# Two transfers per expert chunk move to GpSimd's queue, and three results of the RWKV projections are read one to three turns later

## The chip, the cores and the metric

The kernel runs as one program on one core of one Trainium2 chip. The metric is device time in microseconds of one execution, smaller being better; several executions are timed and their median is given. The engines are named as in the profile: PE (matmul), PEld (its weight loads), DVE, ACT, POOL (GpSimd) and SP; "PEq", "SPq" and so on are their instruction queues.

## The reference

Two transformer-like layers over x of shape (8, 512, 256), float32: eight sequences of 512 tokens with 256 channels. Only the first layer is touched by the change. Cut to what matters:

```python
x = L0_attn_x
xn = _layernorm(x)
x = x + rwkv(xn) + moe(xn)          # layer 0
xn = _layernorm(x)
x = x + attn(xn) + ffn(xn)          # layer 1

def rwkv(x):                        # B=8, T=512, D=256, 16 heads of 16
    dx = conv3(x) - x
    t5 = tanh((x + dx * maa_x) @ maa_w1).reshape(B, T, 5, 32)
    m = einsum('btfc,fcd->fbtd', t5, maa_w2)
    xw, xk, xv, xr, xg = [x + dx * (maa_i + m[i]) for i in range(5)]
    r, k, v, g = xr @ Wr, xk @ Wk, xv @ Wv, silu(xg @ Wg)
    w_log = -exp(time_decay + tanh(xw @ decay_w1) @ decay_w2)
    # S = exp(w)*S + k v^T forward in time, the mirrored recurrence backward
    y = forward_scan(r, k, v, w_log) + backward_scan(r, k, v, w_log)
    y = y * sigmoid(dx @ gate_w + gate_b)
    return group_norm(y) * g @ Wo

def moe(x):                         # 8 experts, 2 per token, hidden 704
    scores = x @ Wg.T
    top, idx = top_k(scores, 2)
    y_e = (silu(x @ W1[e].T) * (x @ W2[e].T)) @ W3[e].T
    return sum of y_e over the token's two experts, times its score
```

## The kernel before, in words

Layer 0 and layer 1 run one after the other; each has its own on-chip pools. In both, the order of the work on PE, DVE, ACT and SP is written out by hand: pieces of work are Python generators, and `Turns.turn()` steps every running generator once, up to its next `yield`. What a generator emits in one turn is put behind what the others emitted in the same turn, and each engine carries its instructions out in that order. A bare `yield` therefore emits nothing and puts all that follows in this generator one turn later, relative to the other generators. POOL alone is not pinned: a scheduler orders its instructions.

Layer 0 begins with `norm_and_route(b)` for the eight sequences (layer norm, router scores, top two), beside `projections(0)`. `place()` then computes for each token its two rows in a table `slots` in DRAM, grouped by expert and cut into 39 chunks of 256 rows, and `scatter()` writes the normalised tokens there with 64 indirect transfers from POOL.

After that three kinds of generators run side by side.

- `scans(turns)` sets the number of turns. It goes over the eight sequences `b`, two channel halves `c` and eight value groups `vg`: 128 steps of four turns each, 512 turns. A step works on a tile `kv` of 128 partitions by 2 by 512: multiply by k (L688), for each of the two values one forward scan (L699) and one backward scan (L703) along time, multiply by r (L708), all on DVE, and, for two steps together, a matmul on PE that sums over the key rows into `ys` (L714). The `kv` tile is loaded by `spread` (L665): eight transfers on SP's queue that read value rows from the DRAM tile `vd` and repeat each on 16 partitions. `kv` has four buffers, and the transfers for step n+1 are written into the program at the start of step n.
- `projections(b + 1)` is added when sequence b begins its scans, and must have filled `made[b + 1]` when they end. It loads the normalised, transposed tokens `xnT` (L485, SP), waits three turns, forms `dx` on DVE (L514 to L516), then projects on PE. `v` goes to DRAM (`vd`, L591, ACT's queue). For the decays, ACT computes `d = exp(-exp(w))` (L620, L621). DVE forms `q = d*d - 1` from it (L626, L627), ACT a first value `near` of 1/q by Ln and Exp (L634, L636), and DVE one Newton step, `dq` (L640, L641), which is scaled (L645, L646). For b of 2 and more, the addition of x in `mixed` (L572) is done on POOL.
- `then(scatter(), experts())`: 32 turns of scatter, then 39 chunks of twelve turns. A chunk gathers expert weights with two indirect transfers from POOL: `wgu` (two buffers) and `wdn` (one buffer). Its tokens `xs` come from `slots` (L396, `load_slots`), are transposed on PE (`turned`, L405) and copied by ACT (`xsT`, L418). PE makes the gate and up products `g` and `u` (L426), ACT applies Silu (L452), DVE multiplies (L435), and PE makes `y` (L465). ACT copies `y` to `ys` (L472), and L473 writes it to the DRAM table `outs`.

`ending(b, c)` normalises and gates the `ys` of a half sequence and, for the second half, multiplies by Wo, adds x and stores it.

Before the change the loads of `xs` are on SP's queue and the stores of `ys` on ACT's queue. In the compiled program the transfers of SP and ACT together take eight completion semaphores in rotation, and those of POOL eight others; a transfer that takes a semaphore first waits until the transfer that had it before has landed. Layer 1, which begins when layer 0's last store has landed, gathers the rows of `outs` per token.

Of the kernel before, what the change touches and what calls it, by code (L numbers as in the profile page):

```python
# [165 lines left out]
def two_layers(ctx: ExitStack, tc: tile.TileContext, a: dict, out: bass.AP):  # L166
    nc = tc.nc
    vec_e, act_e, pool_e, pe = nc.vector, nc.scalar, nc.gpsimd, nc.tensor
# [70 lines left out]
    with ExitStack() as l0:  # L239
# [146 lines left out]
        def weights(i, name, of, n, bufs):  # L386
            w = ew.tile([P, n], F32, tag=name, name=f"{name}_{i}", bufs=bufs)
            pool_e.indirect_dma_start(
                out=w, out_offset=None, in_=of,
                in_offset=bass.IndirectOffsetOnAxis(ap=wrow[:, i : i + 1], axis=0),  # L390
            )
            return w

        def load_slots(i):
            xs = ex.tile([P, NS, D], F32, tag="xs", name=f"xs_{i}", bufs=2)
            nc.sync.dma_start(  # L396
                xs, slots[i * CH : (i + 1) * CH].rearrange("(n p) d -> p n d", p=P)
            )
            return xs

        def turned(i, xs):
            ps = ps_gu.tile([P, NC, CH], F32, tag="gu", name=f"xsT_{i}")
            for c in range(NC):
                for n in range(NS):
                    pe.transpose(  # L405
                        ps[:, c, n * P : (n + 1) * P], xs[:, n, c * P : (c + 1) * P], ident
                    )
            return ps

        def experts():  # L410
            nxt = weights(0, "wgu", a["w0_gu"], GU0, 2)
            ps = turned(0, load_slots(0))
            yield
            for i in range(NCH):
                w, xps = nxt, ps
                wd = weights(i, "wdn", a["w0_dn"], DN0, 1)
                xT = ex.tile([P, NC, CH], F32, tag="xT", name=f"xsT_{i}", bufs=1)
                act_e.copy(xT, xps)  # L418
                if i + 1 < NCH:
                    nxt = weights(i + 1, "wgu", a["w0_gu"], GU0, 2)  # L420
                    xs = load_slots(i + 1)
                yield

                def hidden(o, at):
                    for c in range(NC):
                        pe.matmul(  # L426
                            o, w[:, at + c * P : at + (c + 1) * P], xT[:, c, :],
                            start=c == 0, stop=c == NC - 1,
                        )

                hs = [hpool.tile([P, 2, CH], F32, tag="h", name=f"h_{i}_{j}") for j in range(3)]

                def product(j, g, u):
                    n = 2 - j // 2
                    vec_e.tensor_tensor(hs[j][:, :n, :], hs[j][:, :n, :], u[:, :n, :], ALU.mult)  # L435
                    if n == 1:
                        o = hs[j][64:, 1, :]
                        vec_e.tensor_tensor(o, o, g[64:, 1, :], ALU.mult)

                last = None  # L440
                for j in range(3):
                    g = ps_gu.tile([P, 2, CH], F32, tag="gu", name=f"g_{i}_{j}")
                    hidden(g[:, 0, :], 4 * j * D)
                    hidden(g[:, 1, :], (4 * j + 2) * D)
                    yield
                    if last:
                        product(j - 1, *last)
                    u = ps_gu.tile([P, 2, CH], F32, tag="gu", name=f"u_{i}_{j}")
                    n = 2 - j // 2
                    for k in range(n):  # L450
                        hidden(u[:, k, :], (4 * j + 2 * k + 1) * D)
                    act_e.activation(hs[j][:, :n, :], g[:, :n, :], AF.Silu)  # L452
                    if n == 1:
                        act_e.activation(hs[j][64:, 1, :], g[:64, 1, :], AF.Silu)
                    last = g, u
                    yield
                if i + 1 < NCH:
                    ps = turned(i + 1, xs)
                product(2, *last)
                yield  # L460
                y = ps_gu.tile([P, NS, D], F32, tag="gu", name=f"y_{i}")
                for n in range(NS):
                    for j in range(NJ0 + 1):
                        lo = 64 * (j == NJ0)
                        pe.matmul(  # L465
                            y[:, n, :], hs[j // 2][lo:, j % 2, n * P : (n + 1) * P],
                            wd[lo:, j * D : (j + 1) * D], start=j == 0, stop=j == NJ0,
                        )
                        if j % 3 == 2:
                            yield  # L470
                ys = ex.tile([P, NS, D], F32, tag="ys", name=f"ys_{i}", bufs=1)
                act_e.copy(ys, y)  # L472
                act_e.dma_start(  # L473
                    outs[i * CH : (i + 1) * CH].rearrange("(n p) d -> p n d", p=P), ys
                )

# [3 lines left out]
        def projections(b):  # L480
# [5 lines left out]
                xnT[:, :, PAD : PAD + T], lines[b].rearrange("(c p) t -> p c t", p=P)  # L486
            )
            xT = [xnT[:, c, PAD : PAD + T] for c in range(NC)]
            for _ in range(3):
                yield  # L490

            def shifted(c, s):
# [2 lines left out]
            def big(tag, bufs=2):  # L495
                return rw.tile([P, NC, T], F32, tag=tag, name=f"{tag}_{b}", bufs=bufs)
# [123 lines left out]
                act_e.activation(dT[:, co, :], pss[co], AF.Exp, bias=V("time_decay", co))  # L620
            act_e.activation(dT, dT, AF.Exp, scale=-1.0)  # L621
            yield


            q = rw.tile([P, NC, T + 1], F32, tag="v", name=f"q_{b}", bufs=2)
# [8 lines left out]
                act_e.activation(near[c], q[:, c, :T], AF.Ln, scale=-1.0)  # L634
            for c in range(NC):
                act_e.activation(near[c], near[c], AF.Exp, scale=-1.0)  # L636
            yield
            dq = big("dq")
            for c in range(NC):
# [34 lines left out]
        def scans(turns):  # L674
# [4 lines left out]
            for n, (b, c, vg) in enumerate(todo):  # L679
                if c == vg == 0:  # L680
                    x = rw.tile([P, NT, D], F32, tag="x", name=f"x_{b}")
                    z = rw.tile([P, NC, T], F32, tag="z", name=f"z_{b}")
                    if b + 1 < B:
                        turns.add(projections(b + 1))
# [102 lines left out]
        for b in range(B):  # L787
            nc.sync.dma_start(xns[b], tokens(a["x"][b]))
        turns = Turns()
        first = projections(0)  # L790
        for b in range(B):
            turns.add(norm_and_route(b))
# [10 lines left out]
        place()  # L803
        turns.finish()
        turns.add(then(scatter(), experts()))
        for _ in scans(turns):
            turns.turn()
# [616 lines left out]
```

## Time and profile before

| | us |
|---|---|
| median of 3 runs | 2783.87 |
| lowest and highest | 2782.39, 2789.58 |
| the profiled execution, its time | 2787.46 |
| its span, first to last instruction | 2785.7 |
| PE, PEld, DVE busy | 2359.8, 1402.9, 2137.6 |
| ACT, POOL busy | 870.1, 407.2 |
| mean granted PE clock | 0.919 of full |

The profiled execution's own time is 1.8 us over its span and 3.6 us over the median. The scans and experts of layer 0 fill about 150 to 1480 us of the span, layer 1 the rest from about 1500 us. A busy share is an average over these stages; what a wait in one of them is worth is read from that stage alone.

### The profile page before, as it was taken

The page shows a single profiled execution, that of the slowest core. Times are in us where ns is not written, and L with a number is a line of the kernel's source. Part 1 is how long each engine was busy: PE and PEld are TensorE (multiplying, and loading weights), DVE is VectorE, ACT ScalarE, POOL GpSimd, SP SyncE. Part 2 cuts the span into 40 slices and gives each one's busy share as a digit, 9 for nine tenths or more (in the row PEclk, how much of TensorE's full clock was granted, in tenths as well). Part 3 has the DMA queues.
Part 4 walks back from the last instruction along what each step waited for, and adds up shares of the span by engine and source line. Part 5 has one row for each costly group of instructions (what it writes and reads, how often), then busy time and mean ns, then how long its engine had stood idle before and what let it go on. Part 6 is the DMA issues. An engine that isn't in the chain of part 4 may idle for free.

```text
span 2785.7 us, 32431 instructions
## 1 busy us (share of the span) xinstructions
PE 2359.8 (85%) x11772; PEld 1402.9 (50%) x11772; DVE 2137.6 (77%) x3042; ACT 870.1 (31%) x1649; POOL 407.2 (15%) x368
## 2 busy tenths in 40 slices
PE   4756888988989889898873899999999989998996
PEld 3313555545555555555651445655555545555554
DVE  4698989899999899889894866667576676667656
ACT  1203231232312323122110234444333434343344
POOL 0074121221212112121102110001010100001000
PEclk8768998999999999999895899999998999999998
DMA  8245454445454444544543100010010100000000
GB/s 281 76 147 168 136 169 130 149 131 168 147 164 136 147 149 145 170 118 149 165 128 140 54 28 24 9 35 28 20 31 31 31 28 27 28 20 28 20 9 16
DMA packets 123886, 263.22 MB, mean 94 GB/s; under 512 B 25264, under 2 KB 76368, under 8 KB 118608
## 3 DMA queue, kind: packets, MB, share of 16 engines
q1 hardware_dynamic: 86912, 129.58, 16.4%
q0 software_dynamic: 17376, 103.69, 11.2%
q10 hardware_dynamic: 19440, 27.87, 2.7%
q8 instruction: 95, 1.56, 0.2%
q14 instruction: 63, 0.52, 0.1%
HBM read 215.17 MB, written 45.88 MB: 94 GB/s over the span
## 4 chain that ended last, share of the span: by engine, by line
PE 49%; DVE 26%; DMA 6%; ACT 4%; issue 3%; SPq 2%; POOL 1%; DVEq 0%; ACTq 0%; POOLq 0%
PE y L1307 6%; PE g L1261 5%; PE u L1261 5%; PE y L465 4%; DVE kv L699 4%; PE g L426 3%; DVE kv L703 3%; DMA kv<-vd 3%; PE sc_g L1159 2%; PE u L426 2%; PE o_g L1187 2%; PE ys L714 2%; SPq L665 2%; DVE kv L688 2%; PE qkv_l L1051 1%
## 5 line engine op out<-in xcount | busy, mean ns | idle before, releaser
L703 DVE TENSOR_TENSOR_SCAN kv<-d,kv 128x512 f32<-128x512 f32 x256 | 336.9, 1316 | 8.8
L699 DVE TENSOR_TENSOR_SCAN kv<-dq,kv 128x512 f32<-128x512 f32 x256 | 320.4, 1252 | 2.5
L426 PE MATMUL g<-xsT,wgu 128*128 128x256 f32 x936 | 249.3, 413 | 32.0 <-ACT xsT L418 31.9
L465 PE MATMUL y<-wdn,h 128*128 128x256 f32 x936 | 259.3, 416 | 11.9 <-DVE h L435 11.9
L1167 ACT ACTIVATE pt_g<-sc_g 128x512 f32<-128x512 f32 (+1 forms) x384 | 171.0, 531 | 237.4 <-PE sc_g L1159 202.8
L426 PEld LDWEIGHTS g<-xsT,wgu 128*128 128x128 f32 x936 | 188.3, 207 | 112.1 <-ACT xsT L418 51.4
L465 PEld LDWEIGHTS y<-wdn,h 128*128 128x128 f32 x936 | 173.8, 200 | 111.1 <-issue 76.7
L1261 PE MATMUL g<-xT,w 128*128 128x512 f32 x384 | 199.6, 645 | 24.4 <-DVE h L1296 9.4
L1261 PE MATMUL u<-xT,w 128*128 128x512 f32 x384 | 190.1, 618 | 18.7 <-DVE h L1296 7.6
L426 PE MATMUL u<-xsT,wgu 128*128 128x256 f32 x780 | 192.8, 387 | 0.0
L714 PE MATMUL ys<-kv,cst 128*32 128x512 f32 x512 | 122.1, 638 | 78.3 <-DVE kv L708 78.1
L688 DVE TENSOR_TENSOR kv<-kv,k 128x1024 f32<-128x1024 f32 x128 | 158.1, 1236 | 37.8 <-DMA kv<-vd 22.0
L1307 PE MATMUL y<-w,h 128*128 128x256 f32 x768 | 179.3, 385 | 0.0
L426 PEld LDWEIGHTS u<-xsT,wgu 128*128 128x128 f32 x780 | 151.6, 196 | 37.9 <-issue 14.8
L708 DVE TENSOR_TENSOR kv<-kv,r 128x1024 f32<-128x1024 f32 x128 | 160.8, 1257 | 3.7
L1279 DVE TENSOR_TENSOR h<-h,u 128x512 f32<-128x512 f32 x96 | 66.0, 688 | 120.5 <-PE u L1261 115.9
L1307 PEld LDWEIGHTS y<-w,h 128*128 128x128 f32 x768 | 141.7, 190 | 32.2 <-issue 9.5
L452 ACT ACTIVATE h<-g 128x512 f32<-128x512 f32 (+1 forms) x117 | 61.6, 526 | 287.8 <-PE g L426 280.2
L1173 DVE TENSOR_TENSOR pt_g<-pt_g,cst 128x512 f32<-128x512 f32 x128 | 85.2, 686 | 69.6 <-ACT pt_g L1167 69.5
L1261 PEld LDWEIGHTS g<-xT,w 128*128 128x128 f32 x384 | 72.5, 202 | 108.3 <-issue 83.9
L1167 ACT ACTIVATE pt_l<-sc_l 128x384 f32<-128x384 f32 (+1 forms) x256 | 98.0, 469 | 90.0 <-PE sc_l L1159 71.9
L1173 DVE TENSOR_TENSOR pt_l<-pt_l,cst 128x768 f32<-128x768 f32 (+1 forms) x128 | 107.9, 885 | 14.8 <-ACT pt_l L1167 14.8
(296 smaller groups left out, 3763.4 us busy)
## 6 DMA issues: line engine op xcount, KB each, us to landing
kv<-vd SPq DMA_DIRECT2D x1024, 64.0 KB, 2.7
cb<-cd SPq DMA_DIRECT2D x128, 128.0 KB, 2.9
slots<-zero SPq DMA_DIRECT2D x1, 9984.0 KB, 35.4
xs<-slots SPq DMA_DIRECT2D x39, 256.0 KB, 4.8
outs<-ys ACTq DMA_DIRECT2D x39, 256.0 KB, 2.1
w<-in_w ACTq DMA_DIRECT2D x12, 384.0 KB, 9.5
xn<-in_x SPq DMA_DIRECT2D x8, 512.0 KB, 8.7
xnT<-xT ACTq DMA_DIRECT2D x16, 256.0 KB, 2.1
```

What stands on the lines that cost most here:

```text
L426: pe.matmul(o, w[:, at + c * P : at + (c + 1) * P], xT[:, c, :], start=c == 0, stop=c == NC - 1,)
L465: pe.matmul(y[:, n, :], hs[j // 2][lo:, j % 2, n * P : (n + 1) * P], wd[lo:, j * D : (j + 1) * D], start=j == 0, stop=j == NJ0,)
L688: vec_e.tensor_tensor(kv, kv, bc(kc, 1, NV), ALU.mult)
L699: vec_e.tensor_tensor_scan(out=kv[:, i, :], data0=qc, data1=kv[:, i, :], initial=0.0, op0=ALU.mult, op1=ALU.add,)
L703: vec_e.tensor_tensor_scan(out=kv[:, i, ::-1], data0=dc[:, ::-1], data1=kv[:, i, ::-1], initial=0.0, op0=ALU.mult, op1=ALU.add,)
L708: vec_e.tensor_tensor(kv, kv, bc(rc, 1, NV), ALU.mult)
L714: pe.matmul(y[r0 : r0 + 32, :], C["take"][:, 24 - 8 * at : 56 - 8 * at], kv[:, i, :], start=at == 0, stop=at == 3, skip_group_check=True,)
L1167: act_e.activation(pt[:, i, :end], scs[i][:, :end], AF.Exp, scale=0.25)
L1173: vec_e.tensor_tensor(pt[:, :, a0 : a0 + m], pt[:, :, a0 : a0 + m], bc(mask[:, :m], 1, 4), ALU.mult,)
L1261: pe.matmul(ps, w[:, k, c * P : (c + 1) * P], xT[:, c, :], start=c == 0, stop=c == NC - 1,)
L1279: vec_e.tensor_tensor(hs[-1], hs[-1], u, ALU.mult)
L1307: pe.matmul(y[:, i, :], hs[k][:, (t + i) * P : (t + i + 1) * P], w1[j - 5 + k][:, 2, :], start=k == 0, stop=k == 5,)
```

## The change

Three things are edited, all in layer 0.

1. `load_slots` and the store of `ys` to `outs` are issued by POOL in place of SP and ACT: 39 transfers each.
2. `projections` waits six turns, not three, after it asks for `xnT`, for every sequence but the first.
3. One more `yield` stands between the computation of `d` on ACT and `q` on DVE, and one more between `near` on ACT and the Newton step on DVE.

All arithmetic is the same. `projections(b)` has 41 yields before and 46 after (43 for the first sequence).

```diff
@@ load_slots
             xs = ex.tile([P, NS, D], F32, tag="xs", name=f"xs_{i}", bufs=2)
-            nc.sync.dma_start(
+            pool_e.dma_start(
                 xs, slots[i * CH : (i + 1) * CH].rearrange("(n p) d -> p n d", p=P)
             )
@@ experts
                 act_e.copy(ys, y)
-                act_e.dma_start(
+                pool_e.dma_start(
                     outs[i * CH : (i + 1) * CH].rearrange("(n p) d -> p n d", p=P), ys
                 )
@@ projections
             xT = [xnT[:, c, PAD : PAD + T] for c in range(NC)]
-            for _ in range(3):
+            for _ in range(6 if b else 3):
                 yield
...
             act_e.activation(dT, dT, AF.Exp, scale=-1.0)
             yield
+            yield
...
             q = rw.tile([P, NC, T + 1], F32, tag="v", name=f"q_{b}", bufs=2)
...
             for c in range(NC):
                 act_e.activation(near[c], near[c], AF.Exp, scale=-1.0)
+            yield
             yield
             dq = big("dq")
```

In the instruction lists of the changed program SP has 39 transfers fewer and ACT 39 fewer, and ACT has four fewer loads of a function table (75 for 79). POOL's scheduler puts the new transfers into its queue in a fixed pattern per chunk: the `wdn` of chunk i, the store of chunk i-1, the `wgu` of chunk i+2, the `xs` of chunk i+3. Layer 1's instructions on ACT and DVE are in the same order as before.

## Prediction

> **What bounds the kernel now.** I read the stages first: busy time of each engine in four windows.
>
> ```profile
> core 0: us, PE busy (x) PEld busy (x) DVE busy (x) ACT busy (x) POOL busy (x), PEclk, DMA share, GB/s
> 0.00:240.00 240.00, 134.65 (x368) 63.77 (x368) 175.07 (x322) 45.83 (x64) 86.66 (x84) 0.74 0.47 162
> 240.00:1480.00 1240.00, 1067.33 (x4078) 666.48 (x4078) 1125.34 (x1114) 312.07 (x483) 219.27 (x163) 0.93 0.49 147
> ```
>
> All edits act in the second window, 1240 us long. DVE is the fullest engine there (91%), PE second (86%); POOL and ACT are mostly idle. DVE's idle time, 1240 - 1125 = 115 us, is what can be won while DVE leads. The waits of DVE in that window name 94 us of it:
>
> ```profile
> DVE kv L688 <- DMA kv<-vd: 22.0, 13, 5.0
> DVE kv L688 <- DMA xs<-slots: 15.7, 5, 5.1
> DVE q L626 <- ACT d L621: 11.1, 5, 3.8
> DVE dx L514 <- DMA xnT<-xnT: 10.9, 2, 6.4
> DVE dq L640 <- ACT near L636: 10.7, 6, 2.2
> DVE x L782 <- PE o L777: 8.8, 8, 2.4
> DVE xf L568 <- PE m L563: 8.3, 1, 8.3
> ```
>
> The numbers are total us, times, longest. L688 does not read xs: where it is said to wait for xs, that transfer sat ahead of the kv transfers on SP, so both kv rows are one wait, 37.7 us. Why is kv late? The waits of SP's queue say:
>
> ```profile
> SPq L665 <- DMA outs<-ys: 389.2, 32, 26.0
> SPq L665 <- PE ys L714: 119.0, 26, 16.2
> SPq L396 <- DMA outs<-ys: 70.6, 7, 14.9
> ```
>
> A kv load has nothing to do with the expert output; it waits for it because both rotate through the same eight semaphores. The chain of waits, in order of time, shows one whole case:
>
> ```profile
> 806.04 1.70 PE y L465 x6
> ...
> 807.77 0.59 ACT ys L472
> ...
> 808.38 2.08 DMA outs<-ys
> ...
> 810.48 0.30 SPq L665
> ...
> 810.82 4.18 DMA kv<-vd
> ...
> 815.13 1.24 DVE kv L688
> ```
>
> So once per chunk the scans on DVE hang on the end of PE's expert product, and PE in turn waits for the scans (PE ys L714 on DVE kv L708: 70 us, 36 times). The two fullest engines are tied in a ring.
>
> **What the Trainium skill says.** "DMA: Bandwidth & Descriptors", section "Issuing engines are not separate DMA queues": transfers from SP, ACT and GpSimd run on the same 16 DMA engines, so moving one saves issue time, not bandwidth. The trace fits: DMA share is 0.49, no limit. "SBUF — State Buffer", section "SBUF: two separate sides": a transfer issued by GpSimd has its descriptors written by GpSimd, through a port pair that it shares with DVE, and a holder keeps the pair for a whole instruction. The trace agrees for POOL's arithmetic: beside the POOL addition at 596.45 a scan took 1.93 us, not the median 1.22. It shows nothing of it for POOL's indirect transfers: beside the wgu issue at 615.36 (1.64 us long) DVE's operations keep 1.22 and 0.42. A plain POOL transfer of 256 rows is not in this trace.
>
> **The change part by part.**
>
> *xs and outs leave SP's and ACT's rotation.* SP loses both rows of waits on outs, and 39 issues of 0.42 us. Left in SP's rotation beside kv are vd, xnT, x and after, four transfers per sequence. SP may then run as far ahead as free kv buffers allow: the spread for step n+1 reuses the buffer of step n-3, whose sums were emitted at step n-1 or n-2, and eight issues plus landing take 8 x 0.42 + 2.7 = 6.1 us of a 10.4 us step (512 turns over 147 to 1480 us are 2.6 us each). The waits on vd (48.6 us) and on x (45.0 us, before the store of after) remain on SP with kv queued behind them; each is at most 12 us, about one step, against a lead of one to two steps. Of the 37.7 us I leave 4: 34 won.
>
> *ACT* drops 39 issues of 0.366 us between the copies ys and xsT. PE waits for xsT 24 times, 31.9 us; at some 0.4 us each that falls by 10. It is on the path only where PE leads: credited to PE's slack below, not to the sum.
>
> *POOL* gets 78 issues. The nearest rows, indirect transfers of 128 rows, take 0.94 to 1.94 us each; for 256 rows I bound by 0.94 and twice 1.94, and take the 1.3 of wgu and wdn: 78 x 1.3 = 101 us (73 to 303), inside POOL's 1240 - 219 = 1021 idle us. The store waits for ACT's ys copy; queued behind it are wgu of chunk i+2, xs of chunk i+3, and sometimes an addition xf, a z product or the xnT pads. In front of it stands wdn, which already waits for the same y on PE (377.8 us, 37 times), so the added wait is the copy, 0.6 us, and the issue. wgu is needed 17 turns (44 us) later and lands in 7.8; xs is asked a chunk earlier than before. Only xf can be felt: PE waits for it 5.6 us now, and two turns of cover lie between; an added 3 us fits into 5. What the issues take from DVE is bounded by 0 (an issue that doesn't touch DVE; nothing here could make DVE faster) and 0.7 each, the stretch beside an addition: 0 to 55 us. I take 0, by the wgu issue above.
>
> *First chunk.* xs of chunk 0 now stands behind wdn on POOL. Both lie on the chain at 237 us (scatter, xs, first transposes), where PE stood 14.5 us for it: one issue ahead and its own 1.3 cost +2.5.
>
> *Three extra turns before dx* (10.9 us won of 10.9, the waits being 6.4 and 4.5 against 7.8 of cover). The xnT transfer itself is also freed from the outs waits.
>
> *One turn between d and q, one between near and dq.* Longest waits 3.8 and 2.2, cover 2.6: of 21.8 us I leave 3, so 19 won. Nothing is added to any engine. PE and ACT get the final segments of projections(b) later, turn 46 of 64; the next sequence's first kv is emitted at turn 60, so nobody waits. In the first sequence the two yields fit into the existing turns but for the Silu, which falls behind place(): nothing.
>
> *Sum of DVE waits removed*: 34 + 11 + 19 = 64. Then what is late next: PE. Its own needs in the window are 1067 busy plus its waits that are not on DVE, 31.9 - 10 + 14.5 + 9.5 + 5.6 + 1 = 53: 1120. DVE's are 1240 - 64 = 1176. PE's slack against DVE falls from 120 to 56, about half. DVE's present waits on PE, without the single 8.3 at the first chunk, are 15.7; I take them as doubling with the halved slack: -16. Net 64 - 16 - 2.5 = 45.5. The profiled execution is 2785.7 + 1.8 = 2787.5, so 2742 for a like one; against the median, 2783.9 - 45.5 = **2738**. Layer 1 is emitted as before: 0.
>
> **The rivals.**
>
> *PE takes over.* The clock column is 0.88 to 0.97 in parts of the window, so PE's 1067 is partly slow clock; if in-order PE gives back 40 of 64, the gain is 22: 2762. Against: where PE is densest (510 to 670) the clock is 0.97, as in layer 1, so denser is not slower.
>
> *The kv waits have another origin* (PE ys, 119 us, or vd): then only the turns win, 30 less 8 less 2.5: about 20, 2764. Against: the chain above, and the same steps at 363, 595, 626, 1161 and 1382 us.
>
> *POOL's issues stretch DVE* (slower). 78 plain transfers at 0.7 us of locked-out DVE, as with POOL's additions, are 55 us on the leading engine: 45.5 - 55 = 9 lost, 2793. It decides from 45.5 / 78 = 0.58 us per issue. For: the skill's shared pair, 256 rows where I have only seen 128. Against: the undisturbed operations at 615.
>
> *The whole 64 is kept*, PE's clock rising with its density: 2722.
>
> **How the numbers follow.** 2738 has 0.52, the fully kept gain 0.12, PE 0.15, another origin 0.08, POOL's stretch 0.13. A measurement of this kernel can tell about 0.3%, 8 us. Of the 0.23 for the two small gains 0.02 falls within 8 us, of the 0.13 for the stretch 0.03: faster 0.85, same 0.05, slower 0.10. The range goes from 2706 (every named DVE wait gone, 94, less the 16 given back: 78 won) to 2779 (the small gains at their worst); the stretch is left outside with a little at the lower end.
>
> **What would show it.** Right: no wait of SP on outs; SP's longest rows are PE ys, DVE x and vd; L688's waits under 8 us in all; L626, L640 and L514 near zero; DVE's share in the window up from 91 to about 94%; DVE's waits on PE some 15 us longer. POOL's issues 1 to 2 us. Wrong: scans (L699, L703) with means above 1.32 and 1.25 us; kv waits left; PE waits on POOL xf well over 5.6; or wgu or wdn awaited by PE at all.

## The result and the profile after

The changed kernel takes **2761.84 us** (median of 6 runs, 2756.70 to 2770.33) against 2785.2 us before (6 runs): ratio **0.9919, 95% interval 0.9898 to 0.9939**. It was measured a second time beside the experiments, with 0.9884 (0.9867 to 0.9901), 2759.8 against 2792.1 us. So it is 23 to 32 us faster, where 45.5 were forecast. The direction was right; the gain was half of the forecast by the first measurement and 0.7 of it by the second. As the experiments show, the sum holds two errors that partly cancel: one of its steps, the three turns before `dx`, does not win 10.9 us but costs some 30, and the others win more than forecast.

The window 240 to 1480 us of the changed kernel, columns as in the same view of before:

```profile
240.00:1480.00 1240.00, 1067.90 (x4106) 670.79 (x4104) 1141.72 (x1125) 311.71 (x490) 279.54 (x239) 0.93 0.48 145
```

DVE went from 1125 to 1142 us of 1240, that is 92% and not 94%. POOL has 60 us more. Of the tiles named below, `h` is the experts' product of gate and up, `xf` a mixed input of the projections, `yg` the gated sums of a half sequence, `sd` and `z` belong to its normalisation, and `x` is the sum that `ending` stores. What DVE waits for in this window (total us, times, longest), first rows:

```profile
DVE x L784 <- PE o L779: 24.3, 10, 4.4
DVE h L435 <- PE u L426: 22.3, 5, 14.4
DVE yg L736 <- PE ys L716: 14.6, 9, 2.0
DVE kv L690 <- DMA kv<-vd: 13.9, 4, 5.6
DVE sd L757 <- ACT sd L755: 5.0, 1, 5.0
DVE dq L642 <- ACT near L637: 2.5, 1, 2.5
```

The rows for q and dx are gone, dq is down to one wait. But kv still waits 13.9 us, in four places, and two rows stand high that were next to nothing before: h (2.5 before) and yg (0.5 before). (Of x and sd, some 13 us lie after the last scan, which now comes earlier and so pulls the tail into this window.) What SP's queue waits for:

```profile
SPq L667 <- PE ys L716: 403.7, 59, 27.9
SPq L787 <- DVE x L784: 151.5, 8, 46.0
SPq L667 <- DMA kv<-vd: 89.5, 91, 3.8
SPq L667 <- DMA vd<-v: 76.7, 6, 17.4
```

Both rows on outs (389 and 71 us) have vanished, as said. The last row, six waits on the store of vd, the longest 17.4 us, comes up again below.

In the following, "the scans" are the stretch from the first kv product (L688) to the last (L708): 1330.6 us before, 1313.3 in the changed kernel. The rest after it (1302 to 1312 us in all kernels) is left alone by every edit.

### The profile page after: what moved, and what is told of

It is laid out like the page before. It is cut to its first block, busy times and chain, and to the rows that moved or that the text cites. A ratio compares the mean times of both kernels' runs of the same rounds, so it can differ in the third digit from the quotient of the medians.

```text
span 2768.6 us, 32498 instructions
## 1 busy us (share of the span) xinstructions
PE 2354.6 (85%) x11772; PEld 1404.0 (51%) x11772; DVE 2146.9 (78%) x3042; ACT 861.1 (31%) x1645; POOL 466.3 (17%) x446
## 3 DMA queue, kind: packets, MB, share of 16 engines
q0 software_dynamic: 23616, 124.14, 13.9%
## 5 line engine op out<-in xcount | busy, mean ns | idle before, releaser
L705 DVE TENSOR_TENSOR_SCAN kv<-d,kv 128x512 f32<-128x512 f32 x256 | 335.9, 1312 | 8.8
L701 DVE TENSOR_TENSOR_SCAN kv<-dq,kv 128x512 f32<-128x512 f32 x256 | 328.1, 1282 | 2.7
L690 DVE TENSOR_TENSOR kv<-kv,k 128x1024 f32<-128x1024 f32 x128 | 166.1, 1298 | 13.9 <-DMA kv<-vd 13.9
L1169 ACT ACTIVATE pt_l<-sc_l 128x384 f32<-128x384 f32 (+1 forms) x256 | 98.0, 470 | 90.1 <-PE sc_l L1161 71.9
```

The lines of the kernel that those rows point to most:

```text
L690: vec_e.tensor_tensor(kv, kv, bc(kc, 1, NV), ALU.mult)
L701: vec_e.tensor_tensor_scan(out=kv[:, i, :], data0=qc, data1=kv[:, i, :], initial=0.0, op0=ALU.mult, op1=ALU.add,)
L705: vec_e.tensor_tensor_scan(out=kv[:, i, ::-1], data0=dc[:, ::-1], data1=kv[:, i, ::-1], initial=0.0, op0=ALU.mult, op1=ALU.add,)
L1169: act_e.activation(pt[:, i, :end], scs[i][:, :end], AF.Exp, scale=0.25)
```

## The experiments

Each was timed in five rounds; those run together share the runs of the kernel before (medians of 2784.8 to 2792.1 us). The table is what the text below refers to. "DVE free" is the scans' length less DVE's busy time in it; "kv" and "yg" are DVE's waits there. yg counts the waits for PE's sums and includes one of 2.0 us in the tail after the last scan, except for before and e2; one more wait of yg per trace, for which the trace names no cause, is not in it: 9.6 us in e8, 4.3 in e6, 2.5 in e7. The 26.4 of e5 hold one wait of 10.5 at the first chunk.

| kernel | ratio to before (95%) | scans, us | DVE free | kv | yg |
|---|---|---|---|---|---|
| before | 1 | 1330.6 | 116.6 | 37.7 | 0.5 |
| changed | 0.9919 (0.9898-0.9939) | 1313.3 | 90.1 | 13.9 | 14.6 |
| e8 changed again | 0.9884 (0.9867-0.9901) | 1308.7 | 86.2 | 14.2 | 14.6 |
| e1 transfers alone | 0.9866 (0.9845-0.9888) | 1303.2 | 83.1 | 0 | 2.8 |
| e2 turns alone | 1.0010 (0.9992-1.0028) | 1341.5 | 124.3 | 54.4 | 11.2 |
| e11 outs alone | 0.9875 (0.9851-0.9900) | 1298.9 | 79.1 | 0 | 3.2 |
| e5 transfers + three turns | 0.9926 (0.9908-0.9944) | 1312.8 | 92.8 | 14.6 | 26.4 |
| e12 transfers + one turn before dx | 0.9861 (0.9834-0.9887) | 1299.5 | 75.9 | 5.6 | 3.8 |
| e6 transfers + turn after d | 0.9825 (0.9806-0.9844) | 1285.0 | 66.2 | 0 | 4.7 |
| e7 transfers + turn after near | 0.9825 (0.9807-0.9843) | 1290.2 | 70.3 | 0.7 | 2.8 |
| **e10 transfers + both** | **0.9770 (0.9746-0.9793)** | 1271.5 | 59.9 | 0 | 2.0 |
| e18 outs + both | 0.9790 (0.9770-0.9809) | 1275.8 | 63.2 | 0 | 2.0 |

**Which part wins, which loses.** My theory from the two traces (A) was that the transfers win little (kv) and the turns most. First the transfers without the turns:

```diff
-            nc.sync.dma_start(xs, ...)
+            pool_e.dma_start(xs, ...)
-                act_e.dma_start(outs[...], ys)
+                pool_e.dma_start(outs[...], ys)
```

> The kernel before with its xs loads and outs stores issued by POOL, and none of the added turns. Theory A (the traces of before and after, term by term): the waits of DVE for kv fall from 37.7 us to about 14, which is 24 won; against it stand the first chunk, about 6, and DVE operations stretched beside POOL's operations, about 13: net 5 us faster, 0.998 of before (0.995 to 1.000). Theory B (POOL's plain issues cost as much as they win or more): no gain, 1.000 to 1.006, with kv waits gone all the same and the scans longer. Theory C (the transfers carry the whole result and the turns only move waits about): 20 to 25 us faster, 0.991 to 0.993. In A and B the rows q, dx and dq keep 11, 11 and 11 us of waits, and yg stays under 1 us.

Measured: 37 us faster than before, which is faster than the whole change as first measured (0.9919) and not to be told from its second measurement (0.9884). Theories A and B fell; C came nearest, though the gain is larger than it said. DVE's waits up to 1450 us, first rows:

```profile
DVE q L626 <- ACT d L621: 12.0, 6, 3.8
DVE dq L640 <- ACT near L636: 10.7, 6, 2.2
DVE x L782 <- PE o L777: 9.6, 9, 2.5
DVE h L435 <- PE u L426: 8.6, 7, 2.5
```

There is no row for kv and none for dx: the transfers alone removed all of 37.7 and all of 10.9 us. The load of xnT also goes through SP, so the outs waits had made it late, not too few turns. The three turns had nothing left to win.

The reverse, the turns with xs and outs where they were:

> The kernel before with the added turns alone (three before dx, one after d, one after near), the xs loads on SP and the outs stores on ACT. Theory A: q and dx lose their waits (11.1 and 10.9), dq loses about 9 and yg gains about 12, and PE's ring gives some back: about 10 to 18 us faster, 0.994 to 0.996 of before; kv waits stay at 30 to 40 us. Theory B (POOL's issues ate the gain): the turns alone are as good as or better than the changed kernel, 23 us or more, 0.992 or less. Theory C: under 5 us, 0.998 or more.

No gain at all: q, dx and all but 2.5 us of dq went (30 us), and kv grew by 17, h by 19 and yg by 11. A missed, and so did B; C (under 5 us) held here.

Which of the transfers carries the gain:

> The kernel before with only the outs stores on POOL; xs stays on SP, no turns. Theory A (the waits for semaphores in rotation behind the outs stores are the whole of the transfers' gain): no wait of SP on outs, kv waits under 3 us, time as with both transfers moved, 0.985 to 0.989. Rival (xs on SP, whose load waits for PE's transposes of the chunk before, holds the kv loads behind it up as well): SP waits at the xs line of 30 us or more, kv waits of 8 to 20 us, 0.989 to 0.995.

The outs stores do all of it; xs on POOL or on SP makes no difference that shows. So the step "a kv load waits for the expert's output because both share a rotation" is shown: with outs out of the rotation, kv's waits are zero.

**Which turn loses.** On top of the transfers, one turn at a time, and the changed kernel again beside them:

```diff
-            for _ in range(3):                # e5
+            for _ in range(6 if b else 3):
             act_e.activation(dT, dT, AF.Exp, scale=-1.0)
             yield
+            yield                             # e6
             ...
                 act_e.activation(near[c], near[c], AF.Exp, scale=-1.0)
             yield
+            yield                             # e7
```

> The transfers on POOL and, of the turns, only the three before dx. The transfers alone had no wait on kv and none on xnT left, and took 0.9866 of before; the whole change took 0.9919 and waited 13.9 us for kv in four places. Theory P (the three turns shift the v and k projections and the segments after them against the scans, so that sums on PE stand behind them, and kv buffers come free late): kv waits of 5 us at two to four places, q and dq rows as in the transfers alone, time 0.989 to 0.993 of before. Theory Q (the two turns between ACT and DVE are what costs): no kv waits, 0.985 to 0.988. The prediction's step (three turns win 10.9 us): nothing is left to win, as dx no longer waits.

> The transfers on POOL and, of the turns, only the one between d and q. q's waits, 12.0 us with the transfers alone, go to zero. The prediction's step (the wait is won): 8 to 11 us faster than the transfers alone, 0.983 of before. Theory P (what follows moves one turn, and the wait comes back as others: kv, yg, h): within 5 us of the transfers alone, 0.985 to 0.989. Theory Q: slower than these, 0.989 or more, by yg's waits of 2.0 us per sequence half.

> The transfers on POOL and, of the turns, only the one between near and dq. dq's waits, 10.7 us with the transfers alone, go to under 3. The prediction's step: 8 us faster than the transfers alone, 0.984 of before. Theory A (the dq operations had covered yg, so yg's wait of 2.0 us comes up once per sequence and half): yg 10 to 12 us and no gain, 0.986 to 0.988. Theory Q: slower, 0.989 or more.

> The changed kernel once more, on the chip and beside the runs of these experiments, so that they can be compared: 0.992 of before (0.990 to 0.994), with kv waits of about 14 us in four places and yg waits of about 13 us. If it takes 0.987 here, the difference between it and the transfers alone was one between chips, and the turns cost nothing.

The changed kernel came out at 0.9884 here, below the 0.990 to 0.994 that was expected. So part of its distance to the transfers alone, as first measured, may lie between chips or studies. But e5, beside it on the same chip, stays at 0.9926.

The turns after d and near win 0.41% each (11.4 us). The prediction gave each its own wait. From 240 us on, e7 does take dq's alone (10.7 to 0); e6 takes q's (12.0 to 1.7) and dq's as well (10.7 to 0.5), and h gets 7.4 us longer, so half of what it takes comes back. The three turns lose 0.60% (17 us). DVE's waits with the three turns alone:

```profile
DVE yg L734 <- PE ys L714: 26.4, 11, 10.5
DVE kv L688 <- DMA kv<-vd: 14.6, 4, 5.5
```

These are the two rows of the changed kernel that nobody had ordered (q's waits are gone here and dq's down to 3.9, so the net loss is smaller than these rows). Taking the three turns out of the changed kernel:

> The changed kernel without the three turns before dx; the transfers and the turns after d and after near stay. Each of the two turns took 0.41% off the transfers alone. Theory P (the three turns are what costs): at least as good as the better of the two, 0.979 to 0.983 of before, no kv waits, q and dq both under 2 us. Rival (a shift of one turn is good and one of two or more is not, whichever turns make it): slower than these two, 0.985 to 0.989, with kv, yg or h waits as in the changed kernel.

It takes 2724.8 us, 64 us less than before and some 32 to 35 less than the changed kernel: **the best ratio of all that were tried**. Its waits up to 1415 us:

```profile
DVE h L435 <- PE u L426: 17.0, 10, 7.9
DVE x L784 <- PE o L779: 9.5, 9, 2.5
DVE xf L568 <- PE m L561: 7.0, 5, 2.3
DVE q L627 <- ACT d L621: 1.7, 2, 0.9
```

No kv, no yg, no dq, no dx; the four largest rows sum to 35 us, where before had 94 in all. One thing is not separated from this gain. The mean granted PE clock of the timed runs is 0.927 in e10, against 0.917 in the runs of before beside it, 0.922 in e1 and 0.919 in e8. Within the 17 runs of before beside e13, those at 0.925 took 2778 and 2780 us and those at 0.915 took 2791 to 2793. So some 13 of the 64 us, and some 10 of what e10 has over e8, may go with the clock (an estimate from these runs). Whether e10's schedule raised the clock, or the clock made part of the gain, no run tells.

With xs left on SP it is the same within what can be told:

> Outs stores on POOL, xs loads left on SP, the turn after d and the turn after near, and no turns before dx. The outs stores alone took 0.9875 of before, both transfers 0.9866, so xs's place is worth nothing by itself: within 5 us of the kernel with both, 0.975 to 0.979, no kv waits and 37 POOL issues fewer. Rival (xs on SP stands before kv loads there, and with the tighter schedule its wait for PE reaches them): 0.982 or more, with kv waits of 5 us or more.

**Why the three turns lose: kv.** One reading was that the kv buffers come free too late. A fifth one:

```diff
-kv = rw.tile([P, NV, T], F32, tag="kv", ..., bufs=4)
+kv = rw.tile([P, NV, T], F32, tag="kv", ..., bufs=5)
-xs = ex.tile([P, NS, D], F32, tag="xs", ..., bufs=2)
+xs = ex.tile([P, NS, D], F32, tag=f"xn{i % 2}", ..., bufs=1)
```

> The changed kernel with five buffers for kv and not four; for their room xs_i lies in the space of xn0 and xn1, which are done with before xs_0 is loaded. Theory P (with the three turns, PE has the v and k projections and the expert's y in one row between two pairs of sums, while DVE has little beside its scans and runs ahead; the kv buffer of three steps ago then comes free too late): with one more step of lead the kv waits fall from 14 us to under 2 and the time by 8 to 14 us, to 0.995 to 0.997 of the changed kernel. Rival (DVE is merely ahead of PE there, and the wait moves to the next thing that PE has to give it, yg, h, x or xf): kv waits go, these rows grow by as much, time within 4 us of the changed kernel.

0.9892 (0.9871 to 0.9913), no better than the changed kernel, and the row is as before:

```profile
DVE kv L690 <- DMA kv<-vd: 13.6, 4, 5.4
```

So not the buffers; what I had expected there is refuted. (This run stands beside e10 on the same chip: 34 us lie between the two.) The row of vd in SP's queue gives the next reading. In the changed kernel ACT issues vd's store at 534.4 us (0.37 us). POOL in that moment (start, duration):

```profile
532.33 1.34 POOL L388 DMA_INDIRECT wgu<-in_w_gu,wrow  x1 [4.88 <-PE u L426]
534.51 0.73 POOL L396 DMA_DIRECT2D xs<-slots  x1 [0.84 <-PE xsT L405]
```

SP waits in the meantime (waits of SP from 530 to 545 us):

```profile
SPq L667 <- DMA vd<-v: 17.4, 1, 17.4
```

The timeline of SP and of DVE:

```profile
543.28 5.12 SPq L667 DMA_DIRECT2D kv<-vd  x11
...
547.03 1.23 DVE L690 TENSOR_TENSOR kv<-kv,k 128x1024 f32<-128x1024 f32 x1 [5.59 <-DMA kv<-vd]
```

vd's 512 KB leave in the same microseconds as the expert's next weights and slots; SP's wait ends 8.9 us after the issue, and the kv load behind it in the rotation reaches DVE 5.6 us late. In e10 the same store is issued at 521.9, well ahead of POOL's next load (first the row of issues, with KB and us to landing, then POOL's timeline, then SP's and DVE's):

```profile
vd<-v ACTq DMA_DIRECT2D x1, 512.0 KB, 2.8
```

```profile
527.59 1.03 POOL L388 DMA_INDIRECT wgu<-in_w_gu,wrow  x1 [16.25 <-PE u L426]
```

```profile
524.77 14.34 SPq L667 DMA_DIRECT2D kv<-vd  x18
...
537.50 1.84 DVE L690 TENSOR_TENSOR kv<-kv,k 128x1024 f32<-128x1024 f32 x1
```

It lands in 2.8 us. The experiment takes vd's store out of the rotation, once with the three turns and once without:

```diff
-            act_e.dma_start(vd.rearrange("(c p) t -> p c t", p=P), v)
+            pool_e.dma_start(vd.rearrange("(c p) t -> p c t", p=P), v)
```

> The changed kernel, three turns included, with the store of vd issued by POOL as well, so that it leaves the rotation in which kv loads wait. Theory R (the store of vd falls, with the three turns, on the same moment as the wgu and xs transfers, lands some 9 us and not 2.8 us after its issue, and SP's kv loads stand behind it): kv waits fall from 14 us to under 3 and the time by 7 to 14 us, to 0.984 to 0.987 of before; yg keeps its 13 us. Rival (PE's sums free the kv buffer late, or the wait moves on to x and h): kv waits of 10 us or more stay, or x and h grow by as much, and the time is the changed kernel's within 4 us, 0.988 to 0.992.

> The two transfers and the two turns (0.977 of before, no kv waits) with the store of vd on POOL as well. Theory R: there is no kv wait to win, so the time stays within 4 us of 0.977, 0.9755 to 0.9785. Rival (moving vd is worth something by itself, through ACT's queue or SP's, apart from the three turns): 7 us or more faster, under 0.9745.

With the turns: 0.9862 (0.9837 to 0.9886), scans 1290.0 us (18.7 less than in e8, whose ratio of 0.9884 is not clearly above), and no kv row:

```profile
DVE h L435 <- PE u L426: 20.9, 7, 14.4
DVE yg L736 <- PE ys L716: 11.3, 8, 2.0
DVE x L784 <- PE o L779: 8.2, 7, 3.3
```

Without them: 0.9796 (0.9772 to 0.9819), no gain over e10. So the waits for kv came from vd's store in the rotation. But the collision with the weight loads is only half of it. SP waits as long for vd where DVE doesn't wait for kv at all; in e10 (240 to 1415 us):

```profile
SPq L667 <- DMA vd<-v: 78.9, 6, 15.4
```

What differs is the lead: the time from the end of SP's wait for vd to the moment at which DVE is ready for the kv tile whose load stood behind it. In the lines above it is 524.8 to 537.5 in e10, and 543.3 to 541.4 (547.03 less 5.59) in the changed kernel. From the timelines, for the six stores after 340 us (e12, e15 and e16, described further below, have other numbers of turns):

| kernel | turns added before dx | lead, us | kv waits |
|---|---|---|---|
| e10 | 0 | 9.0 to 12.8 | 0 |
| e12 | 1 | 8.1 to 10.0 | 5.6 |
| changed | 3 | 3.7 to 5.4 in four, -1.8 and -1.0 in two | 13.9 |
| e16 | 8 | 9.8 to 12.8 | 0 |
| e15 | 12 | 11.2 to 16.4 | 0 |

Three turns (7.8 us) later, the store stands about that much nearer to a kv load that DVE soon needs. What lead is left then goes where a transfer meets the weights: twice by the store itself (8.8 and 8.0 us, waits of 5.6 and 4.5), and twice by the kv loads behind it, which land in up to 6.5 us and not 2.1 beside wdn, though the store took its 2.8 (waits of 1.5 and 2.3). In e12 it is kv loads beside wgu and xs that land in up to 9.6 us. Late stores alone do no harm: two in e10 land in 6.4 and 6.7 us, two in e15, beside wgu and xs, in 6.8 and 7.0, and DVE doesn't wait. A step is four turns, and eight and twelve turns are whole steps; that fits the table. This account was read from the traces after the runs, and none was made to test it.

**Why the three turns lose: yg.** Before the yg product DVE has this in the changed kernel:

```profile
571.31 0.42 DVE L435 TENSOR_TENSOR h<-h,u 128x256 f32<-128x256 f32 x1 [2.13 <-PE u L426]
571.76 0.42 DVE L438 TENSOR_TENSOR h<-h,g 64x256 f32<-64x256 f32 x1
574.21 0.69 DVE L736 TENSOR_TENSOR yg<-sig,ys 128x512 f32<-128x512 f32 x1 [2.02 <-PE ys L716]
```

and this in e10, in another sequence:

```profile
717.66 0.69 DVE L627 TENSOR_SCALAR q<-d 128x1026 f32<-128x1026 f32 x1
718.38 1.23 DVE L628 SCALAR_TENSOR_TENSOR q<-d,q 128x1026 f32<-128x1026 f32 x1
719.52 1.22 DVE L690 TENSOR_TENSOR kv<-kv,k 128x1024 f32<-128x1024 f32 x1
720.77 0.69 DVE L736 TENSOR_TENSOR yg<-sig,ys 128x512 f32<-128x512 f32 x1
```

The two q operations, 1.9 us, stand just ahead of yg and give PE the time for its last sums; in before and e1 it is the four dq operations that stand there. With the three turns neither does, and yg waits 1.5 to 2.02 us in six sequences. Two runs on this. The first theory, that the turn after near had uncovered yg, was tested by taking that turn out of the changed kernel:

> The changed kernel without the added turn between near and dq; the rest of the change stays. Theory A (this turn only moved its wait: the four dq operations, 4 x 0.7 us in front of yg on DVE, had covered yg's wait for the sums on PE): yg's waits fall from 12 us to under 1, those of dq come back to about 9 to 11, and the time is that of the changed kernel within 5 us (0.998 to 1.002 of it). The prediction's own step (the turn is worth its 9 us): 8 to 10 us slower than the changed kernel, with yg's waits as they are there.

0.9945 (0.9929 to 0.9962): yg's waits stayed at 13.9 us, so this turn was not the cause; and dq got 28.3 us of waits, 17.7 of them in one place at the first chunk. Then yg got a turn more:

```diff
             nc.sync.dma_start(x, tokens(a["x"][b]))
+            yield
             yg = rw.tile(...)
```

> The changed kernel with one more turn ahead of yg in ending. Theory A (yg waits 2.02 us, once per sequence and six times in all before the last, since its last sums on PE come too late): yg's waits in the window fall from 12.6 us to under 3 and the time falls by 5 to 10 us against the changed kernel, 0.996 to 0.998 of it. Rival (the turn puts the chain yc, var, rs, z and the release of the one ys buffer later, so that PE waits there, and DVE and PE meet elsewhere): the row yg goes and PE's waits on DVE grow by as much; the time is within 3 us of the changed kernel or longer.

> The changed kernel, three turns included, with both losses taken away that the traces name: vd's store on POOL (kv waits 14 us, gone in e13) and one more turn ahead of yg (yg waits 13 us). If the three turns cost by these two waits, the time is 11 us below the kernel with vd's store on POOL alone, which took 0.9862 of before: 0.981 to 0.984, against 0.977 without the three turns; what is left over of the distance, some 12 us, are DVE's operations stretched beside POOL's and the first chunk's h. Rival (yg's wait only moves on to h, x or z): 0.985 or more, with these rows longer by 10 us.

On the changed kernel 0.9865 (0.9845 to 0.9884): below its first measurement by more than forecast, not clearly below its second. The yg row went, h rose to 29.0 and z to 4.6. On e13, 0.9847 (0.9824 to 0.9871): the scans get 5.4 us shorter, while yg's row gives up all 11.3; h and x took 11 us of it again (26.0 and 14.3). Most of yg's wait moved on, and the two ratios can't be told apart. Both remedies together do not reach e10: 1284.6 us of scans against 1271.5.

**Why the three turns lose: DVE's own time.** The rest is not a wait. The operations on kv take 1.22 us each when undisturbed. Between 145 and 1415 us, those that took over 1.3 us lay, one and all, beside an addition xf or a product z on POOL, and exceeded 1.22 by, in sum:

| before | e1 | e10 | e18 | e5 | changed | e13 |
|---|---|---|---|---|---|---|
| 39.0 | 46.7 | 39.2 | 39.3 | 45.3 | 53.0 | 52.8 |

A case of the changed kernel, POOL and DVE:

```profile
702.21 0.73 POOL L396 DMA_DIRECT2D xs<-slots  x1
702.96 2.15 POOL L572 TENSOR_TENSOR xf<-xf,xnT 128x512 f32<-128x512 f32 x2
...
702.41 3.79 DVE L701 TENSOR_TENSOR_SCAN kv<-dq,kv 128x512 f32<-128x512 f32 x1
```

One scan lasts as long as an issue and two additions that stand behind one another. In before the longest was 2.22 us. e10 has POOL issue 36 loads of xs and 39 stores of outs between 240 and 1470 us as well, and no more stretch than before in sum, though single scans are held longer there too: one for 4.55 us beside four additions in a row, three for 2.8 to 2.9 beside an issue with a product behind it. An issue alone cost nothing: of the kv operations of e10 beside an issue with no POOL arithmetic, 212 in number, the mean is 1.22 us and the longest 1.25. That it is where the additions fall is read from the traces; no run moved the additions by themselves. The three turns on top of the transfers alone did not add to the sum (46.7 in e1, 45.3 in e5); they did so only together with the two other turns.

**Is it the place or the number of turns?**

> The transfers on POOL and one more turn before dx (four, from the second sequence on) in place of three more. Theory P with a place in the order (what counts is where the v and k projections fall between the pairs of sums, which come every eight turns): one turn leaves them on the good side, no or few kv waits, 0.982 to 0.988 of before. Rival (any turn before dx costs, as all of what follows comes later): between the transfers alone and the three turns, 0.988 to 0.991, kv waits of 4 us or more.

One turn in place of three: 0.9861, the transfers' own time within what can be told. The waits of q and dq were gone (0.7 and 0.5 us), and h (21.4) and kv (5.6) had come. Two larger numbers on e10, `range(15 if b else 3)` and `range(11 if b else 3)`:

> The two transfers and the two turns, with twelve more turns before dx from the second sequence on. A chunk of the experts takes twelve turns (30.9 us, at 2.6 us a turn), so vd's store falls at the same place of a chunk as without any. Theory R (place against the experts' chunk decides): no kv waits over 2 us in all, 0.976 to 0.980. Rival (later is worse, by the number of turns): kv waits and yg waits beyond those of the three turns, 14 and 13 us, and 0.988 or more.

> The same with eight more turns before dx: the period of the pairs of sums on PE, but four turns off the experts' chunk, one more than the three of the change. Theory R: as with the three turns, vd's store meets a wgu or xs load in some sequences and kv waits of 5 to 15 us come back, 0.982 to 0.990. Rival (the place against the pairs of sums decides): as without the extra turns, no kv waits, 0.976 to 0.980.

0.9901 (0.9877 to 0.9924) and 0.9952 (0.9937 to 0.9967), both with no kv wait. For twelve turns that is what the place against the chunk said of kv; for eight it is not. So the place against the chunk alone doesn't decide on kv; the lead, above, fits both. And the times missed in both: twelve turns brought waits of xf (28.2, one of 20.6 at the first chunk) and z (17.9), eight turns of h (41.1, one of 17.3 at the first chunk). Neither the chunk's period nor that of the sums makes a shift free. What decides on the whole time for an arbitrary shift stays open; no turns before `dx` was the best of the numbers tried.

## Why the prediction was right and wrong

**The bound and the ring: right.** DVE's idle time was what could be won. In e10 the scans fell by 59 us, of which 57 are DVE's free time (116.6 to 59.9).

**xs and outs: right, a little small.** 34 were forecast; all 37.7 of kv went and SP's waits on outs with them. The 10.9 of dx belong here too: the text said that xnT is freed from the outs waits as well, and then booked the wait under the turns.

**The turns after d and near: right.** 19 forecast, 27 measured with the transfers (0.9866 to 0.9770 of some 2790 us). By the intervals of the two ratios this is known to some 9 us, so the forecast isn't clearly too small.

**The three turns before dx: this is the step that failed.** "10.9 us won of 10.9" measured as a loss of 32 us (0.9884 in e8, against 0.9770 without them in e10; against e9, beside e10, 34 us), and as a loss of 17 us on the transfers alone (e5 against e1). The step counted the cover that dx gains and nothing of what follows: each later instruction of the projections moves too, and meets other neighbours. By the traces of the changed kernel and e10, the loss consists of kv 13.9 us (the store of vd nearer to the loads behind it, and beside the weight loads), yg some 12.6 without the tail (its cover, q, moved past it), 13.8 of longer DVE operations (beside POOL's additions), and some 7 at the first chunk (16.9 us of waits between 236 and 260 against 9.9). These 47 stand against 42 us between the lengths of the scans (1313.3 and 1271.5); the small rows (x +6.6; xf -5.0; h elsewhere, z and q together -4.5) take off some 3. The profiled run of the changed kernel was its longest of six (2770.3 us); with e8's profile the difference is 37 us. That the three turns cost is shown by runs, and that kv's waits come through the rotation; the shares of yg and of the longer operations are read from the traces (of yg's, the one run that took it away won 5.4 us of scans, e17).

**"Each is at most 12 us, about one step, against a lead of one to two steps": wrong.** Both halves failed. SP's waits for vd grew to 17.0 us with the transfers alone (e1), where none reached DVE. With the three turns they are hardly longer than that (17.4 and 16.6 us in two sequences), but the lead was down from 9 to 13 us to 5.4 us and less, and 5.6 and 4.5 reached DVE. The 4 us left for kv was 13.9.

**PE's slack, -16: about right for e10, half of what the changed kernel shows.** DVE's waits on PE for h, x, xf and yg grew in e10 by about 13 (h +14.5, x +0.7, xf -1.8, yg -0.5), and in the changed kernel, tail left out, by 31 (h +19.8, x +7.3, yg +12.1, xf -8.4).

**POOL's issues: size wrong, conclusion right for the issues.** 0.73 and 0.74 us each, not 1.3. Stretch taken as 0: it is 0.2 us in e10, 7.7 in e1 and 14 in the changed kernel, every time beside additions or products, never beside an issue alone. PE's waits for POOL's xf rose from 5.6 to 12.4 (6.6 in e8's profile), past what the prediction named as a sign against it.

**First chunk, +2.5: can't be told.** What was priced is PE's wait for the first xs, 14.5 us before. It is 10.4 in e1 and 17.2 in e10, and 19.3 and 14.0 in two profiles of the changed kernel, so one trace doesn't settle 2.5 us. DVE's waits there are 8.3 before, 5.5 in e1, 9.9 in e10 and 16.9 in the changed kernel.

**The rivals.** "PE takes over" named 2762, the measured time, by a mechanism that didn't decide: without the three turns nothing like 40 us was given back, so the match is luck. "The whole 64 is kept", 2722, is what e10 measured at 2724.8, by other terms than those in its sum and without the three turns; the clock did rise, as it said, but its share is not known. "Another origin" is refuted for before by e1 and e11; what is left of kv's waits in the changed kernel does come from vd. "POOL's issues stretch DVE" as priced, 55 us, is refuted by e10 (75 issues, 0.2 us) and e1 (76 issues, 7.7 us).

## What to carry to other kernels

A wait for semaphores in rotation ties transfers that have nothing to do with each other; find the one whose producer is late, here the outs stores, move that one, and see what is left before giving more lead to loads that merely stood behind it. A step that is put off by some turns moves all that follows it: list for each later instruction what it stood in front of (it may have been another's cover), what its transfers will meet and how much lead they have over their reader (here waits of 15 us in a queue cost nothing where the lead was 9 us and more), and what two instructions of a helper engine now stand behind one another. Where a change has several parts, time them apart: here one part of five lost half of what the others won.

## What the runs showed of the hardware

- A direct transfer of 256 KB issued by POOL takes it 0.73 to 0.74 us. In the changed kernel it lands later than through SP or ACT before: xs in 7.2 us (median) against 4.8, outs in 6.2 against 2.1. How much of this is the queue and how much the weight loads that POOL issues next to it is not separated: through SP, xs landed in 3.1 in e11. PE waited for xs once, at the first chunk (19.3 us, 14.5 before).
- A store of 512 KB on ACT's queue landed in 2.8 us by itself; with wgu issued 2.1 us before it and xs 0.1 us after, SP's wait for it ended 8.9 us after its issue.
- An issue on POOL alone did not lengthen DVE's operations on kv: 212 of them beside one in e10 took 1.22 us in the mean, 1.25 at most. POOL additions in a row held a scan for 3.79 us (two behind an issue, changed kernel) and 4.55 us (four, e10) in place of 1.22.
